# Two transformer layers on one core: loads in order of use, three dense units instead of four, scatters of two units in turn, the last row's slot rows made in one go

## The chip, the cores and the metric

The kernel runs on one core of a Trainium2 chip. The metric is the device time of one execution in microseconds (us). A core has five engines that work beside each other: TensorE (PE, matrix products; its weight loads are listed as PEld), VectorE (DVE), ScalarE (ACT), GpSimd (POOL) and SyncE (SP), which here does nothing but issue DMA transfers. SP, ACT and POOL each have a queue of their own for the transfers that they issue. POOL alone issues the indirect ones: scatters and gathers by a list of row numbers.

## The reference

The input is x, four rows (batch entries) of 1024 tokens with 128 numbers each, in float32. Two layers are applied; each adds an attention and a mixture of experts to x, both computed from the same normalised x:

```python
x = L0_attn_x
xn = _layernorm(x, axis=-1)
x = x + _L0_attn_ref(xn, ...) + _L0_ffn_ref(xn, ...)
xn = _layernorm(x, axis=-1)
x = x + _L1_attn_ref(xn, ...) + _L1_ffn_ref(xn, ...)
return x
```

The first layer's attention has 16 query heads of 8 numbers and one key/value head. Its "ffn" is itself an attention, with 8 heads (H) of width 128 (P), whose values and outputs each come from 8 experts (E):

```python
gate_v = _get_sel_gate(x, sel_v_w, rs)   # sigmoid, the best 2 of 8, normalised, times route_scale
gate_o = _get_sel_gate(x, sel_o_w, rs)
q = jnp.einsum('bsd,hpd->bhsp', x, q_w.reshape(H, P, D))
k = jnp.einsum('bsd,hpd->bhsp', x, k_w.reshape(H, P, D))
xv = jnp.einsum('bsd,hedp->bshep', x, v_w.reshape(H, E, D, P))
v = jnp.einsum('bshep,bshe->bhsp', xv, gate_v)
att = jax.nn.softmax(jnp.einsum('bhqp,bhkp->bhqk', q, k) * SCALE, axis=-1)
ctx = jnp.einsum('bhqk,bhkp->bqhp', att, v)
weighted = ctx[:, :, :, None, :] * gate_o[..., None]
out = jnp.einsum('bshep,hepd->bsd', weighted, o_w.reshape(H, E, P, D))
```

Since a gate is zero for six of the eight experts, only two of the eight values of a token and head are needed.

The second layer has a linear attention (16 heads, 64 random features, FAVOR+) and an ordinary mixture of experts: a router picks 2 of 8 experts per token, each expert is 128 to 512, exact gelu, 512 to 128, and a shared expert of the same size is added for every token.

## The kernel before

**Units.** The first layer's expert attention is cut into 32 units, u = 8 b + h, one for each row b and head h. The loop over u (L1055) has an inner loop over n = 0 to 7 (L1057), one step for each 128 query tokens. A step writes the scores' two 128x512 products (ss, L940), their maximum (DVE, L945) and exponential (ACT, L947), transposes an earlier step's probabilities (pTp, L960, copied by DVE, L964, and ACT, L966), makes half of the context at n = 4 and at n = 0 of the next unit (cp, L972), and writes outputs: two products against eight experts (po, L993), each weighed by the output gates on DVE (g_o, L997), then summed over the experts by add_experts (DVE 128x512, L824; POOL 128x256, L825) and two more POOL additions (L1002, L1003). The first attention's work (attend(): mx L613 with its maximum nmh L619, sT L667, pT L674, ov L657) is woven between these.

**Values, dense.** The first DENSE = 4 units, all of row 0, compute the values of all eight experts for every token: switch_values (L827) makes two 128x512 products for each n (pv, L835), DVE multiplies each by the gates (gv, L839), add_experts adds the first half to the second on DVE (L824) and the quarters on POOL (L825), and a last POOL addition (L844) writes vs. All of g_o, gv and two other temporaries take turns in three buffers (tag "gs"). Unit 0's values are made in one burst at u = 0, n = 3; those of unit u + 1 during unit u by the table VALUES (at u = 0: four n at step 4, then LATER).

**Values, sorted.** The other 28 units compute only the two chosen experts. 16 scatters (8 n x 2 choices, L864, POOL) put each token's normalised row into sorted_v[u % 4] at a place that the tables give, so that tokens of one expert stand together. Groups of four 128-token blocks are then loaded by SP (group_load, L870, which also fetches each block's expert weights), transposed (xvT, L892) and multiplied (pg, L897 on), written to DRAM by SP, gathered back by 16 POOL transfers (L916) and combined with their gates by POOL (L931, L932). A unit's scatters are spread over the two units before it by the table PAIR (L1016), which serves two units at a time (v and v + 1, where v is u + 3 at odd and u + 2 at even u): within one step all scatters of the first unit come before all of the second. group_load of a unit starts two units ahead, at step 4. The places in sorted_v that no token takes must be zero: four transfers of 1.47 MB at the start clear the four buffers (L1046 to L1050).

**Startup.** The loads of L97 to L151 stand on SP's queue in the order of the text: x of row 0, the two halves of sel, rs, wq, four pieces of bq, wk, then 9 pieces of bk0 and 9 of keep, wv, bv, wo, bo; after them the q and k weights of unit 0 (load_scores(0), L1036) and its value weights (load_dense(0), L1037), the other rows of x (L1044), and the clears. The layernorm of row 0, its transposes (lnT, L240) and copies by ACT into xnT (L241), the product qkT (L801) and the queries qks (L816) are the first compute.

**Last row.** Between the layers each token's normalised row is scattered with its number and its share to sorted_x at the place of its expert, once for each of two choices (slot_rows, L328): for each, POOL normalises 128 tokens into a buffer xslot, of which there are two (L334), copies the token number (L339) and the share (L340), and scatters (L341). For rows 0 to 2 this happens during the units of the following rows. For row 3 it is the end of last_row (L1292): the row's layernorm, router, the tables of all experts, then slot_rows. last_row runs as an "aside", advanced twice for every step of the second layer's attention (L1749 to L1764); a "filler" beside it gives the shared expert for three rows, then drains what is left of the aside, then the experts, whose first act is to load the sorted tokens (xg, L1655; transposed at L1670). wide() (L1288) is a pool of seven buffers that the second layer uses.

**Order.** PE, SP and POOL run in the order of the text in the first layer; DVE and ACT are ordered by a scheduler. In the second layer only PE and SP keep the order of the text (L1174).

## Time and profile before

| | before |
|---|---|
| three plain runs, us | 3378.05, 3382.25, 3383.11 (median 3382.25) |
| the profiled execution, us | 3353.22 |
| its span, us | 3351.2 |
| mean granted TensorE clock | 0.975 of full speed |
| instructions | 48567 |
| DMA moved | 293.65 MB, 88 GB/s on average |

The profiled execution is one of its own, 29 us below the median of the plain ones; stages and durations below come from it. The units of the first layer run until about 2860 us of the span, the second layer from there to the end.

A line of the part with the groups of instructions reads so:

```profile
L864 POOL DMA_INDIRECT sorted_v<-xv,gates x448 | 446.8, 997 | 387.4 <-DMA sorted_v<-xv,gates 322.4
L825 POOL TENSOR_TENSOR g_o<-g_o 128x256 f32<-128x256 f32 x256 | 191.7, 749 | 459.6 <-DVE g_o L824 430.3
L997 DVE TENSOR_TENSOR g_o<-po,go 128x512 f32<-128x512 f32 x512 | 334.0, 683 | 44.3 <-POOL x L1003 21.9
```

The first is: line 864 of the kernel, on POOL, an indirect DMA that writes sorted_v from xv by numbers in gates, 448 times; busy 446.8 us in all, 997 ns each; before them POOL stood idle for 387.4 us, of which 322.4 ended when an earlier scatter into sorted_v landed. The busy time of a DMA instruction is what the issuing engine spends on it, not the transfer. A row of the windows has a stretch of the span, its length, the busy time (and the number of instructions) of PE, PEld, DVE, ACT and POOL in it, the granted clock, the share of the DMA engines' time, and GB/s. A row of the waits has engine, line, what it waited for, the total in us, how often, and the longest. A row of the timeline has start, duration, engine, line, instruction, and in brackets the engine's idle time before it and what ended it.

### The profile page before, as it was taken

The page shows a single profiled execution, that of the slowest core. Times are in us where ns is not written, and L with a number is a line of the kernel's source. Part 1 is how long each engine was busy: PE and PEld are TensorE (multiplying, and loading weights), DVE is VectorE, ACT ScalarE, POOL GpSimd, SP SyncE. Part 2 cuts the span into 40 slices and gives each one's busy share as a digit, 9 for nine tenths or more (in the row PEclk, how much of TensorE's full clock was granted, in tenths as well). Part 3 has the DMA queues.
Part 4 walks back from the last instruction along what each step waited for, and adds up shares of the span by engine and source line. Part 5 has one row for each costly group of instructions (what it writes and reads, how often), then busy time and mean ns, then how long its engine had stood idle before and what let it go on. Part 6 is the DMA issues. An engine that isn't in the chain of part 4 may idle for free. (4 is left out here: it accounts for less than half of the span.)

```text
span 3351.2 us, 48567 instructions
## 1 busy us (share of the span) xinstructions
PE 3161.5 (94%) x15286; PEld 1712.1 (51%) x15286; DVE 2450.3 (73%) x4726; ACT 1817.6 (54%) x3164; POOL 1865.9 (56%) x2351
## 2 busy tenths in 40 slices
PE   5899999999999999999899999999999999879998
PEld 3344544555545444555454455555455554447776
DVE  7998777776788767676878786767666645648886
ACT  2234555555555555555555555556556566346665
POOL 1344355666657666666467667765767644153333
PEclk9999999999999999999999999999999999889999
DMA  4122443433322223333132232332333220024445
GB/s 141 48 65 76 131 140 98 123 104 96 87 74 84 86 76 96 93 94 92 57 94 88 86 90 89 99 92 82 97 88 92 85 77 13 12 64 88 86 91 133
DMA packets 449333, 293.65 MB, mean 88 GB/s; under 512 B 41450, under 2 KB 422260, under 8 KB 449076
## 3 DMA queue, kind: packets, MB, share of 16 engines
q1 hardware_dynamic: 404884, 221.32, 23.5%
q0 software_dynamic: 41952, 68.16, 7.4%
q8 instruction: 122, 2.00, 0.2%
q10 hardware_dynamic: 2240, 1.07, 0.1%
q14 instruction: 135, 1.11, 0.1%
HBM read 176.29 MB, written 113.71 MB: 87 GB/s over the span
## 5 line engine op out<-in xcount | busy, mean ns | idle before, releaser
L619 DVE TENSOR_REDUCE nmh<-mx 128x1 f32<-128x512 f32 x1024 | 664.2, 682 | 272.8 <-PE mx L613 271.2
L864 POOL DMA_INDIRECT sorted_v<-xv,gates x448 | 446.8, 997 | 387.4 <-DMA sorted_v<-xv,gates 322.4
L674 ACT ACTIVATE pT<-sT 128x512 f32<-128x512 f32 x1024 | 557.2, 600 | 164.4 <-PE sT L667 94.2
L940 PE MATMUL ss<-xnT,qTs 128*128 128x512 f32 x1024 | 493.4, 604 | 7.1 <-DVE g_o L997 2.6
L945 DVE TENSOR_REDUCE nms<-ps 128x1 f32<-128x1024 f32 x256 | 311.0, 1215 | 255.1 <-ACT ps L943 254.0
L972 PE MATMUL cp<-pTs,vs 128*128 128x512 f32 x1024 | 458.9, 602 | 21.2 <-DVE pTs L964 18.1
L993 PE MATMUL po<-ow,cTs 128*128 128x512 f32 x1024 | 474.4, 596 | 0.7 <-ACT cTs L977 0.7
L825 POOL TENSOR_TENSOR g_o<-g_o 128x256 f32<-128x256 f32 x256 | 191.7, 749 | 459.6 <-DVE g_o L824 430.3
L943 ACT COPY ps<-ss 128x512 f32<-128x512 f32 x512 | 299.4, 586 | 254.0 <-PE ss L940 250.9
L947 ACT ACTIVATE ps<-ps,nms 128x1024 f32<-128x1024 f32 x256 | 294.4, 1150 | 159.2 <-DVE nms L945 158.1
L997 DVE TENSOR_TENSOR g_o<-po,go 128x512 f32<-128x512 f32 x512 | 334.0, 683 | 44.3 <-POOL x L1003 21.9
L667 PE MATMUL sT<-qs,ks 75*128 75x512 bf16 x1024 | 310.6, 384 | 13.2 <-DVE nmh L619 9.3
L613 PE MATMUL mx<-ks,qs 72*128 72x512 bf16 x1024 | 312.9, 383 | 10.7 <-DVE nmh L619 4.9
L972 PEld LDWEIGHTS cp<-pTs,vs 128*128 128x128 f32 x1024 | 192.8, 193 | 245.7 <-issue 229.5
L960 PE MATMUL pTp<-ident,ps 128*128 128x128 f32 x2048 | 273.9, 277 | 12.5 <-ACT ps L947 8.8
L940 PEld LDWEIGHTS ss<-xnT,qTs 128*128 128x128 f32 x1024 | 190.1, 192 | 186.4 <-issue 105.1
L960 PEld LDWEIGHTS pTp<-ident,ps 128*128 128x128 f32 x2048 | 243.2, 143 | 81.4 <-issue 17.4
L993 PEld LDWEIGHTS po<-ow,cTs 128*128 128x128 f32 x1024 | 179.7, 191 | 158.8 <-issue 127.4
L977 ACT COPY cTs<-cp 128x512 f32<-128x512 f32 x64 | 37.4, 585 | 409.2 <-PE cp L972 403.0
L916 POOL DMA_INDIRECT vs<-yv,gates x224 | 219.2, 979 | 67.1 <-issue 56.1
L916 POOL DMA_INDIRECT yg<-yv,gates x224 | 216.6, 967 | 68.3 <-issue 68.0
L657 PE MATMUL ov<-pT,va 128*32 128x512 f32 x2048 | 248.4, 603 | 0.0
(314 smaller groups left out, 4826.8 us busy)
## 6 DMA issues: line engine op xcount, KB each, us to landing
vb<-in_v_w_dram SPq DMA_DIRECT2D x644, 64.0 KB
xs<-sorted_v SPq DMA_DIRECT2D x140, 256.0 KB
yv<-xs SPq DMA_DIRECT2D x140, 256.0 KB
w<-in_w_dram SPq DMA_DIRECT2D x78, 256.0 KB
sorted_x<-nobody SPq DMA_DIRECT2D x16, 1040.0 KB
ow<-in_o_w_dram SPq DMA_DIRECT2D x32, 512.0 KB
qs<-qd SPq DMA_DIRECT2D x144, 64.0 KB
sorted_v<-xv,gates POOLq DMA_INDIRECT x448, 2.3
```

Of the source, the lines that this page charges most:

```text
L613: nc.tensor.matmul(sc, lhsT=qs[0:NPAIR, i, ts(n, P)], rhs=ks[0:NPAIR, ts(kc, 512)], start=True, stop=True,)
L619: nc.vector.tensor_reduce(halves[:, i, n, kc : kc + 1], sc, axis=AX.X, op=ALU.max)
L667: nc.tensor.matmul(sc, lhsT=ks[:, ts(kt, P)], rhs=qs[:, i, ts(c, 512)], start=True, stop=True,)
L674: nc.scalar.activation(pT, sc, AF.Exp)
L864: nc.gpsimd.indirect_dma_start(out=sorted_v[u % 4][:, :], out_offset=bass.IndirectOffsetOnAxis(ap=column(u, k, n).bitcast(I32), axis=0), i ...
L916: nc.gpsimd.indirect_dma_start(out=to[:, n, :], out_offset=None, in_=unit[u, "y"][:, :], in_offset=bass.IndirectOffsetOnAxis(ap=column(u, ...
L940: nc.tensor.matmul(sc, lhsT=qT[:, ts(n, P)], rhs=xnT[b][:, ts(c, 512)], start=True, stop=True)
L945: nc.vector.tensor_reduce(nm, p, axis=AX.X, op=ALU.max, negate=True)
L960: nc.tensor.transpose(pt[:, ts(k, P)], p[:, ts(4 * k4 + k, P)], ident)
L972: nc.tensor.matmul(cp, lhsT=v[:, kt, :], rhs=pT[:, kt, :], start=(kt == 0), stop=(kt == NT - 1),)
L993: nc.tensor.matmul(po, lhsT=cT[:, ts(qt, P)], rhs=unit[u, "ow"][:, ts(c, 512)], start=True, stop=True,)
L997: nc.vector.tensor_tensor(g[:, ts(c, 4), :], po.rearrange("p (e c) -> p e c", e=4), bcast(go[:, ts(c, 4)], P), ALU.mult,)
```

## The change

- **Loads.** After x of row 0, the order on SP is now: q and k weights of unit 0, the two halves of sel (load_gates), wq, wk, the odd pieces of bk0 and keep, wv, bv, wo, bo (load_small), the value weights of unit 0. rs, the four pieces of bq and the pieces of bk0 and keep with even j (6 of bk0 and 6 of keep) are issued by ACT.
- **Dense units.** DENSE is 3: unit 3 is sorted. In the three dense units DVE weighs the first product of each n as before; the second is weighed by ACT, four instructions of 128x128 with a scale per token. The first addition of add_experts is done by POOL for the values of units 0 and 1, by DVE for unit 2 and for all outputs. The values of unit 2 are made at steps 1 to 4 of u = 1, two n per step.
- **Scatters.** Unit 3's 16 scatters are issued in the first four steps of u = 1, four each; PAIR_1 places those of units 4 and 5 in u = 1 and 2. From then on PAIR holds as before, but within a step the scatters of the two units alternate.
- **Last row.** last_slots makes row 3's slot rows: eight DVE instructions and one ACT copy into two wide buffers, four POOL copies for all token numbers and shares, and then 16 scatters, one for each advance of the aside. The aside is advanced three times per step for the first 15 advances and two times after.

```diff
@@ -42,3 +42,3 @@
 VG = 4
-DENSE = 4
+DENSE = 3
 
@@ -111,22 +111,7 @@
     sel = fixed([P, 2 * SH * SE], "sel")
-    nc.sync.dma_start(sel[:, 0 : SH * SE], a["sel_vT"])
-    nc.sync.dma_start(sel[:, SH * SE :], a["sel_oT"])
     rs = fixed([P, 1], "rs")
-    nc.sync.dma_start(rs, a["route_scale"].unsqueeze(0).to_broadcast([P, 1]))
+    wq0, bq0 = fixed([P, D], "wq0"), fixed([P, 1], "bq0")
 
-    wq0 = fixed([P, D], "wq0")
-    nc.sync.dma_start(wq0, a["Wq0T"])
-    bq0 = fixed([P, 1], "bq0")
-    for g in range(NG):
-        nc.sync.dma_start(
-            bq0[ts(g, 4 * HD), :], a["bq0"][:, :, g].rearrange("i d -> (i d)").unsqueeze(1)
-        )
-
-    wk0 = fixed([P, NSTACK], "wk0")
+    wk0, bk0 = fixed([P, NSTACK], "wk0"), fixed([NSTACK, 1], "bk0")
     nc.gpsimd.memset(wk0[:, NPAIR:], 0.0)
-    nc.sync.dma_start(
-        wk0[:, 0:NPAIR].rearrange("e (r d) -> e r d", d=HD),
-        a["Wkv0T"][:, 0:HD].unsqueeze(1).to_broadcast([P, NPAIR // HD, HD]),
-    )
-    bk0 = fixed([NSTACK, 1], "bk0")
     nc.gpsimd.memset(bk0, 1.0)
@@ -137,16 +122,32 @@
     nc.gpsimd.memset(minus1, -1.0)
-    for i in range(NPART):
-        for j in range(NPART):
-            r = 24 * i + HD * j
-            nc.sync.dma_start(bk0[r : r + HD, :], a["bkv0"][0:HD].unsqueeze(1))
-            for k in range(j):
-                nc.sync.dma_start(keep[r : r + HD, k : k + 1], minus1[0:HD, 0:1])
-    wv0 = fixed([P, HD], "wv0")
-    nc.sync.dma_start(wv0, a["Wkv0T"][:, HD : 2 * HD])
-    bv0 = fixed([P, HD], "bv0")
-    nc.sync.dma_start(bv0, a["bkv0"][HD : 2 * HD].unsqueeze(0).to_broadcast([P, HD]))
-    wo0 = fixed([P, D], "wo0")
-    nc.sync.dma_start(wo0, a["Wo0T"])
-    bo0 = fixed([P, D], "bo0")
-    nc.sync.dma_start(bo0, a["bo0"].unsqueeze(0).to_broadcast([P, D]))
+    wv0, bv0 = fixed([P, HD], "wv0"), fixed([P, HD], "bv0")
+    wo0, bo0 = fixed([P, D], "wo0"), fixed([P, D], "bo0")
+
+    def load_gates():
+        nc.sync.dma_start(sel[:, 0 : SH * SE], a["sel_vT"])
+        nc.sync.dma_start(sel[:, SH * SE :], a["sel_oT"])
+        nc.scalar.dma_start(rs, a["route_scale"].unsqueeze(0).to_broadcast([P, 1]))
+
+    def load_small():
+        nc.sync.dma_start(wq0, a["Wq0T"])
+        nc.sync.dma_start(
+            wk0[:, 0:NPAIR].rearrange("e (r d) -> e r d", d=HD),
+            a["Wkv0T"][:, 0:HD].unsqueeze(1).to_broadcast([P, NPAIR // HD, HD]),
+        )
+        for g in range(NG):
+            nc.scalar.dma_start(
+                bq0[ts(g, 4 * HD), :],
+                a["bq0"][:, :, g].rearrange("i d -> (i d)").unsqueeze(1),
+            )
+        for i in range(NPART):
+            for j in range(NPART):
+                r = 24 * i + HD * j
+                queue = (nc.scalar, nc.sync)[j % 2]
+                queue.dma_start(bk0[r : r + HD, :], a["bkv0"][0:HD].unsqueeze(1))
+                for k in range(j):
+                    queue.dma_start(keep[r : r + HD, k : k + 1], minus1[0:HD, 0:1])
+        nc.sync.dma_start(wv0, a["Wkv0T"][:, HD : 2 * HD])
+        nc.sync.dma_start(bv0, a["bkv0"][HD : 2 * HD].unsqueeze(0).to_broadcast([P, HD]))
+        nc.sync.dma_start(wo0, a["Wo0T"])
+        nc.sync.dma_start(bo0, a["bo0"].unsqueeze(0).to_broadcast([P, D]))
 
@@ -323,3 +324,3 @@
         yield from weigh(comb[:, b, :, 0:ME], oh0, share[:, 0, b, :], oh1, share[:, 1, b, :])
-        to_slots[b] = slot_rows(b, at_slot)
+        to_slots[b] = slot_rows(b, at_slot) if b < B - 1 else (moments[1, b], at_slot)
 
@@ -821,5 +822,5 @@
 
-        def add_experts(g):
+        def add_experts(g, engine):
 
-            nc.vector.tensor_tensor(g[:, 0:4, :], g[:, 0:4, :], g[:, 4:8, :], ALU.add)
+            engine.tensor_tensor(g[:, 0:4, :], g[:, 0:4, :], g[:, 4:8, :], ALU.add)
             nc.gpsimd.tensor_tensor(g[:, 0:2, :], g[:, 0:2, :], g[:, 2:4, :], ALU.add)
@@ -838,7 +839,16 @@
                 )
-                nc.vector.tensor_tensor(
-                    g[:, ts(c, 4), :], pv.rearrange("p (e c) -> p e c", e=4),
-                    bcast(gates[b][:, n, ds(h * SE + 4 * c, 4)], P), ALU.mult,
-                )
-            add_experts(g)
+                if c == 0:
+                    nc.vector.tensor_tensor(
+                        g[:, 0:4, :], pv.rearrange("p (e c) -> p e c", e=4),
+                        bcast(gates[b][:, n, ds(h * SE, 4)], P), ALU.mult,
+                    )
+                else:
+                    for e in range(4, SE):
+                        i = h * SE + e
+                        nc.scalar.activation(
+                            g[:, e, :], pv[:, ts(e - 4, P)], AF.Copy,
+                            scale=gates[b][:, n, i : i + 1],
+                        )
+
+            add_experts(g, nc.gpsimd if u < 2 else nc.vector)
             nc.gpsimd.tensor_tensor(v[:, n, :], g[:, 0, :], g[:, 1, :], ALU.add)
@@ -1000,3 +1010,3 @@
                 )
-            add_experts(g)
+            add_experts(g, nc.vector)
             nc.gpsimd.tensor_tensor(g[:, 0, :], g[:, 0, :], g[:, 1, :], ALU.add)
@@ -1012,3 +1022,3 @@
         LATER = {5: (4,), 6: (5,), 7: (6, 7)}
-        VALUES = {2: (0,), 3: (1, 2), 4: (3,), **LATER}
+        VALUES = {1: (0, 1), 2: (2, 3), 3: (4, 5), 4: (6, 7)}
 
@@ -1019,2 +1029,7 @@
         )
+
+        PAIR_1 = (
+            (0, 0, 0, 0, 3, 3, 3, 3, 1, 1, 1, 1, 0, 0, 0, 0),
+            (0, 0, 0, 0, 0, 0, 0, 0, 2, 2, 2, 2, 2, 2, 2, 2),
+        )
         GATHER = {13: (0,), 14: (1,), 15: (2,), 16: (3, 4), 17: (5,), 18: (6, 7)}
@@ -1036,2 +1051,4 @@
         load_scores(0)
+        load_gates()
+        load_small()
         load_dense(0)
@@ -1130,7 +1147,19 @@
                 v = u + 3 if odd else u + 2
+                if u == 1 and n < 4:
+                    for i in range(4 * n, 4 * n + 4):
+                        scatter(DENSE, i)
                 if u > 0 and v < U:
-                    for k, counts in enumerate(PAIR):
+
+                    pair = []
+                    for k, counts in enumerate(PAIR_1 if u < 3 else PAIR):
                         done = sum(counts[: n + 8 * (1 - odd)])
-                        for i in range(done, done + counts[n + 8 * (1 - odd)]):
-                            scatter(v + k, i)
+                        pair.append([
+                            (v + k, i)
+                            for i in range(done, done + counts[n + 8 * (1 - odd)])
+                        ])
+                    pair.sort(key=len, reverse=True)
+                    for i in range(len(pair[0])):
+                        for of_unit in pair:
+                            if i < len(of_unit):
+                                scatter(*of_unit[i])
 
@@ -1154,3 +1183,3 @@
                     for k in list(to_slots):
-                        if k < B - 1 and next(to_slots[k], to_slots) is to_slots:
+                        if next(to_slots[k], to_slots) is to_slots:
                             del to_slots[k]
@@ -1291,2 +1320,31 @@
 
+    def last_slots(moments_b, at_slot):
+
+        mv, rstd = moments_b
+        b = B - 1
+        to = [
+            wide(f"xlast{k}")[:, 0 : NT * ROW].rearrange("p (n d) -> p n d", d=ROW)
+            for k in range(2)
+        ]
+        for n in range(NT):
+            nc.vector.tensor_scalar(
+                to[0][:, n, 0:D], x[b][:, n, :], mv[:, n, 0:1], rstd[:, n : n + 1],
+                ALU.subtract, ALU.mult,
+            )
+        nc.scalar.copy(to[1][:, :, 0:D], to[0][:, :, 0:D])
+        for k in range(2):
+            nc.gpsimd.tensor_copy(
+                to[k][:, :, D].bitcast(I32), token[:, b * NT : (b + 1) * NT]
+            )
+            nc.gpsimd.tensor_copy(to[k][:, :, D + 1], share[:, k, b, :])
+        yield
+        for n in range(NT):
+            for k in range(2):
+                nc.gpsimd.indirect_dma_start(
+                    out=sorted_x[:, :],
+                    out_offset=bass.IndirectOffsetOnAxis(ap=at_slot[:, k, n : n + 1], axis=0),
+                    in_=to[k][:, n, :], in_offset=None,
+                )
+                yield
+
     def last_row():
@@ -1297,3 +1355,3 @@
         yield
-        yield from to_slots[B - 1]
+        yield from last_slots(*to_slots[B - 1])
 
@@ -1749,3 +1807,3 @@
     filler = fill()
-    due = 0.0
+    due, taken = 0.0, 0
     for k, (rows_now, rate) in enumerate((
@@ -1756,4 +1814,5 @@
         for _ in run(*its):
-            next(aside, None)
-            next(aside, None)
+            for _ in range(3 if taken < 15 else 2):
+                next(aside, None)
+                taken += 1
             due += rate
```

## Prediction

> **What bounds the kernel now.** I read the totals and the slices first, then the busy time by stage, then what TensorE (PE) waited for, and last the timeline of the three places that the change touches.
>
> ```profile
> PE 3161.5 (94%) x15286; PEld 1712.1 (51%) x15286; DVE 2450.3 (73%) x4726; ACT 1817.6 (54%) x3164; POOL 1865.9 (56%) x2351
> PE   5899999999999999999899999999999999879998
> DVE  7998777776788767676878786767666645648886
> ```
>
> PE is busy 94% of the span, so only 190 us of idle PE can be won, plus whatever PE work is removed. The slices show where it idles: the first two (168 us) and the last rows before the experts (slices 35 and 36).
>
> ```profile
> 0.00:84.00 84.00, 49.46 (x148) 25.75 (x149) 62.51 (x139) 18.48 (x30) 14.35 (x45) 0.92 0.49 141
> 84.00:168.00 84.00, 70.47 (x204) 31.17 (x203) 75.83 (x164) 20.81 (x36) 27.79 (x42) 0.94 0.17 48
> 168.00:252.00 84.00, 76.59 (x254) 37.78 (x253) 78.41 (x141) 26.04 (x44) 39.85 (x56) 0.96 0.20 65
> 252.00:336.00 84.00, 79.91 (x314) 38.31 (x312) 70.63 (x117) 39.17 (x71) 41.39 (x57) 0.96 0.27 79
> 2000.00:2500.00 500.00, 495.43 (x2315) 256.74 (x2315) 349.32 (x657) 296.16 (x543) 336.31 (x423) 1.00 0.31 91
> 2900.00:3000.00 100.00, 77.03 (x411) 41.89 (x410) 47.51 (x132) 41.96 (x50) 38.50 (x70) 0.81 0.12 35
> ```
>
> Columns: stretch, its length, busy PE, weight loads, DVE, ACT, POOL, then granted clock, DMA share, GB/s. Until 252 us DVE is as full as PE or fuller (75.8 and 78.4 of 84 in the second and third rows), ACT is a quarter busy: there DVE sets the pace, and PE idles 34.5+13.5+7.4 = 55 us. At 2000 us PE has 495 of 500: nothing but less PE work helps there.
>
> ```profile
> PE cp L972 <- DVE pTs L964: 18.1, 10, 5.3
> PE xgT L1670 <- DMA xg<-sorted_x: 13.7, 2, 12.0
> PE qkT L801 <- DMA qk<-in_q_wT_dram: 8.8, 1, 8.8
> POOL sorted_v L864 <- DMA sorted_v<-xv,gates: 322.4, 183, 5.3
> ```
>
> Total, times, longest. The first is DVE's lateness in the dense units, the second the last row's scatters, the third the startup load, the fourth scatters that wait for the one before into the same tensor.
>
> **Loads in order of use.**
>
> ```profile
> 7.07 0.80 SPq L143 DMA_DIRECT2D keep<-minus  x1
> 18.50 0.43 SPq L774 DMA_DIRECT2D qk<-in_q_wT_dram  x1
> 21.25 0.72 PE L801 MATMUL qkT<-ident,qk 128*128 128x128 f32 x2 [8.84 <-DMA qk<-in_q_wT_dram]
> 23.76 3.75 PE L816 MATMUL qks<-xnT,qkm 128*128 128x512 f32 x4 [0.47 <-DVE qkm L809]
> ```
>
> The weights of unit 0 are issued at 18.5 behind the small loads, and land 2.75 us later. Issued just behind x, they land before the layernorm's transposes end (12.4), so the whole 8.84 could go. But 12 of the little bk0/keep loads go to ACT ahead of its two copies of xnT (11.43 and 12.45 to 13.04), and each waits for an earlier DMA of its lane, four at a time. A DMA's way from issue to landing is 2.3 (the scatters' row) to 2.75 (qk): after rstd (ends 9.47) two such rounds and four issues of 0.45 make 6.4 to 7.3, so the first copy starts at about 16.3 and qks at about 17.2: -6.5. Smallest gain -4 (one more round), greatest -8.8 (the whole wait). SP sends the same number of bytes as before; the four clears of sorted_v (1.47 MB each, 16.09 us of issue from 23.92) move about 9 us earlier and lie behind the same unit 0 work, whose x and weights are ahead of them.
>
> **Dense units: half to ACT, adds of units 0 and 1 to POOL.** From DVE go 24 multiplies of 0.68 (L839) = 16.3, and 16 adds of 0.76 (L824) = 12.2. ACT gains 96 instructions of 128x128; the only row of that shape, mk L1427, takes 0.31: 29.8 us where ACT is 25% busy, hidden; were it not, about 1.2 per n against 0.68 saved. POOL gains 16 adds 128x512 of 1.06 (L931) to 1.37 (L932 where gaps are dense): 17 to 22 us. Unit 0's eight n come in one burst: on DVE 8 x 2.12 = 17 us before; on POOL now 8 x (1.37+0.75+0.48) = 21. POOL is then the slow one in that burst, so its gain is small: I take -3 for all of u = 0 on top of the startup, 0 to -8 (half of DVE's 23 us for units 0 and 1, less the POOL surplus).
>
> The Trainium skill's page "SBUF — State Buffer", section "Who interferes with whom", speaks against this step: a DVE instruction with two SBUF inputs contends with a GpSimd one that reads SBUF, and the loser waits it out. The trace's row for such a DVE add, L824, is 643/683/3127 ns (least, median, most) while POOL is over half busy, so a block exists but is rare. By the rule 16 POOL adds of 1.37 could cost DVE 22 us and the step would be worth nothing; by the row the cost is near 1 us. I go by the row.
>
> **Unit 3 sorted instead of dense.** PE loses 16 matmuls of 0.86 = 13.8 us and gets six groups of 1.33 (transposes and products of sorted blocks) = 7.9: -5.9, in a part that is 95% PE-busy (fourth row): it counts nearly in full, -6. From DVE go 16 x 0.68 + 8 x 0.76 = 17 us, partly beyond PE's bound: 0 to -8 more; I take -1. POOL gets 16 scatters (one DMA each), 16 gathers of 0.97 and 2 combines (2 x 1.06 + 1.37), SP the group loads and the yv writes of unit 3. In u = 2 and 3 POOL has room (41 of 84).
>
> **The scatters in u = 1** are the price.
>
> ```profile
> 149.50 1.21 POOL L864 DMA_INDIRECT sorted_v<-xv,gates  x1 [0.17 <-issue]
> 152.22 0.96 POOL L864 DMA_INDIRECT sorted_v<-xv,gates  x1 [1.51 <-DMA sorted_v<-xv,gates]
> 153.49 1.08 POOL L864 DMA_INDIRECT sorted_v<-xv,gates  x1 [0.30 <-issue]
> ```
>
> A scatter into the tensor of the one before starts 0.97 + 1.51 = 2.48 later; into another tensor 0.97 + 0.30 = 1.27. In u = 1 there are now 16 for unit 3 and 12 for unit 4, each in a row of its own tensor: 28 x 2.48 = 69. POOL also has eight output tails (0.72+0.46+0.45 = 1.7 each, 13.6) and the eight tails of unit 2's values (0.75+0.48, 9.9): 93 us. u = 1 lasted 149.5 to 246 = 96.5, with DVE full; DVE now has 8 x 0.68 = 5.4 less, so 91. POOL becomes the bound at about 93 to 98 (steps 1 to 3 need 9.9 + 1.7 + 2.5 = 14.1 against 12 on average; later steps 9.1 don't give that back when DVE needs 11): the change in u = 1 is 0, between -4 and +6. Queued behind the scatters on POOL are the g_o and gv sums, which free the three buffers that DVE's multiplies write, which free PE's po and pv banks. On SP the first group load of unit 3 (step 4) waits for the sixteenth scatter, and the qs and nmT loads of the first attention (L597, L643) lie behind it.
>
> **Scatters in turn, from u = 3.** They save up to 183 waits of about 1.2 on POOL, but PE is 99% busy there and waits for POOL nowhere for more than 1 us: 0, at best -4 (row changes).
>
> **The last row.**
>
> ```profile
> 2946.26 1.09 POOL L341 DMA_INDIRECT sorted_x<-xslot,at_slot  x1 [0.98 <-DMA sorted_x<-xslot,at_slot]
> 2949.57 1.09 POOL L341 DMA_INDIRECT sorted_x<-xslot,at_slot  x1 [1.11 <-DMA sorted_x<-xslot,at_slot]
> 2987.78 0.66 PE L1670 MATMUL xgT<-ident,xg 128*128 128x128 f32 x2 [12.01 <-DMA xg<-sorted_x]
> ```
>
> Sixteen scatters go from 2932.6 to 2982.9, 3.3 apart, and each already waits about 1 us for the one before to land: the slot row (0.79+0.18+0.17) is hidden in that wait. They all still go into sorted_x, so making the rows ahead takes nothing off while the landing stays at 3.2; at the 2.48 of L864 it takes 15 x 0.8 = 12. On the other side the first scatter now waits for eight DVE instructions, an ACT copy (0.58 to 1.15) and four POOL copies (0.18 each): 8 x 0.27 + 1 + 0.7 = 4, and for the DVE work queued ahead of them, about 3: +4 to +7. Taking the aside three per step brings the chain forward by 0 to 5. Net 0, between -12 and +6.
>
> **Sum.** -6.5 - 3 - 7 + 0 + 0 + 0 = -16.5, on the profiled 3353.2 (span 3351.2): 3336.7. The three plain runs have the median 3382.25, 29 above it, so the forecast is 3382.25 - 16.5, about 3366. A change within 0.2%, 6.8 us, can't be told from none.
>
> **Rivals.**
> 1. POOL takes over in u = 1 outright and the change is slower. The scatters of that stage (84 to 260 us) land after 2.2 to 3.4 us, median 2.8. If the spacing is 3.4, POOL needs 28 x 3.4 + 23.5 = 119, +22; with SP's loads held behind the group load for one more step (+8) that is +30, less the 16.5 of the sum: +13, 3395. It decides from a spacing of about 2.9. Against it: the measured spacing in this stage is 2.7 and 2.48. Chance 0.22.
> 2. The gains before u = 1 are all handed back, since POOL is the last in u = 1 whatever comes before it, and only unit 3's PE work counts, against a last row that starts 6 late: -6.5 + 6 + 0, 3382. For: 93 against 91 is near. Against: POOL can only start its scatters when u = 1 starts, so an earlier start stays. Chance 0.14.
> 3. Everything pays: startup -8.8, u = 0 -8, unit 3 -8, the last row -6: -31, 3351. For it: PE idles 55 us in the first 252. Chance 0.12.
> 4. The ready slot rows do not do what they say: the chain keeps its 3.3 and starts 6 late. Alone that gives 3382.25 - 16.5 + 6 = 3372, inside the forecast case, so it has no chance of its own.
>
> **How the numbers follow.** The forecast case, 3357 to 3375, has 0.52. Faster is it and case 3, 0.64; same 0.14; slower 0.22. The range goes from 3352 (case 3) to 3390 (most of the way to case 1).
>
> **What would show it.** In the changed profile: PE's first qks at about 17 instead of 23.8, and xnT copies behind ACT's DMA issues; the first scatter of u = 1 near 140 instead of 149.5; u = 1 with POOL over 90% busy and a wait of DVE or PE for POOL's sums; one pass less of PE work for unit 3 before 340; the last row's scatters still over 3 apart and xgT near 2972, the same 16 early. I am wrong if u = 1 takes over 105 us, if the last row's scatters fall to 2.5 apart, or if PE's idle time between 60 and 260 does not fall.

## The result

The changed kernel takes 3371.39 us (median of 13 runs, 3365.72 to 3379.76), the kernel before beside it 3386.09 (13 runs). The ratio is 0.9964 with a 95% interval of 0.9951 to 0.9976: -12.2 us, between -16.6 and -8.1. The forecast was -16.5.

The profiled execution of the changed kernel has a span of 3368.5 us, longer than the 3351.2 of the profile shown before. That earlier profile was quicker than any of the 13 runs beside it: a second profile of the same kernel has a span of 3383.9 (run before_again). The two agree within 0.2 us on the start of unit 5 (521.0 and 520.8 us), and within 0.5 us on the second layer (562.6 and 562.1 from the start of unit 31); the 33 us lie between, where the change touches nothing but the order of the scatters. So stages are compared below up to unit 5 and from unit 31 on, and the stretch between them, where one kernel differs by more than the change is worth, with caution.

The page of the changed kernel, totals and two of the slice rows:

```profile
PE 3174.4 (94%) x15323; PEld 1718.9 (51%) x15323; DVE 2417.9 (72%) x4670; ACT 1852.0 (55%) x3273; POOL 1897.1 (56%) x2345
...
PE   6889999999999999999899999999999999889998
...
DVE  6787786767778767666868876667666655658886
```

Against the first profile of the kernel before, PE is busy for 13 us more, against the second (3176.4) for 2 less, at nearly the same clock (0.973 and 0.972): of the 6 us of PE work that the forecast took away little is to be seen. DVE has 32 us less than in the first profile, ACT 34 more, POOL 31 more. The windows of the same kernel (columns as before: stretch, length, PE, PEld, DVE, ACT, POOL, clock, DMA share, GB/s):

```profile
0.00:84.00 84.00, 52.27 (x160) 27.88 (x160) 58.59 (x135) 29.37 (x64) 22.75 (x53) 0.89 0.56 152
84.00:168.00 84.00, 73.73 (x196) 32.80 (x195) 66.33 (x137) 30.68 (x71) 41.81 (x53) 0.88 0.14 38
168.00:252.00 84.00, 74.24 (x260) 40.05 (x259) 71.52 (x127) 33.95 (x73) 46.44 (x62) 0.92 0.26 82
252.00:336.00 84.00, 78.10 (x344) 40.51 (x343) 60.37 (x101) 45.39 (x83) 42.46 (x52) 0.94 0.45 131
```

DVE is relieved as planned (66.3 instead of 75.8 in the second row, 71.5 instead of 78.4 in the third), POOL takes it over (41.8 instead of 27.8), and PE is busy for 6 us more in the first two rows together and 4 less in the last two: a new wait has come in, and the granted clock is lower (0.88 instead of 0.94, 0.92 instead of 0.96). The waits of the changed kernel:

```profile
PE lnT L241 <- DVE xn L234: 17.3, 4, 10.8
...
PE cp L982 <- DVE pTs L974: 10.3, 9, 2.7
...
PE pTp L970 <- DVE gv L841: 8.5, 2, 6.8
...
PE xgT L1728 <- DMA xg<-sorted_x: 2.4, 2, 2.2
```

The wait for qk (8.8) is gone, the one for the sorted tokens is down from 13.7, and a single wait of 6.8 for a multiply of values by gates (gv) has come.

### The profile page after: what moved, and what is told of

Same layout as the page of the kernel before. It is cut to its first block, busy times and chain, and to the rows that moved or that the text cites. A ratio compares the mean times of both kernels' runs of the same rounds, so it can differ in the third digit from the quotient of the medians.

```text
span 3368.5 us, 48933 instructions
## 1 busy us (share of the span) xinstructions
PE 3174.4 (94%) x15323; PEld 1718.9 (51%) x15323; DVE 2417.9 (72%) x4670; ACT 1852.0 (55%) x3273; POOL 1897.1 (56%) x2345
## 5 line engine op out<-in xcount | busy, mean ns | idle before, releaser
L874 POOL DMA_INDIRECT sorted_v<-xv,gates x464 | 466.1, 1005 | 334.0 <-DMA sorted_v<-xv,gates 247.1
L970 PEld LDWEIGHTS pTp<-ident,ps 128*128 128x128 f32 x2048 | 242.6, 143 | 90.4 <-issue 18.3
L926 POOL DMA_INDIRECT vs<-yv,gates x232 | 228.5, 985 | 67.5 <-issue 59.4
L926 POOL DMA_INDIRECT yg<-yv,gates x232 | 224.2, 967 | 73.7 <-issue 73.4
```

Of the source, the lines that this page charges most:

```text
L874: nc.gpsimd.indirect_dma_start(out=sorted_v[u % 4][:, :], out_offset=bass.IndirectOffsetOnAxis(ap=column(u, k, n).bitcast(I32), axis=0), i ...
L926: nc.gpsimd.indirect_dma_start(out=to[:, n, :], out_offset=None, in_=unit[u, "y"][:, :], in_offset=bass.IndirectOffsetOnAxis(ap=column(u, ...
L970: nc.tensor.transpose(pt[:, ts(k, P)], p[:, ts(4 * k4 + k, P)], ident)
```

## The experiments

Twelve runs followed, in three groups on three chips (A, B, C); each is compared with the kernel before on its own chip (3386.2 us, 3387.2 and 3364.5). On which chip the changed kernel and the first profile ran is not on record. "Start of a unit" is the start of DVE's first row maximum (nms) in it, read from the traces:

| kernel | chip | ratio to before (95%) | us | unit 1 starts | unit 2 | unit 5 |
|---|---|---|---|---|---|---|
| before (first profile / before_again) | - / B | 1 | 0 | 148.5 / 148.3 | 234.0 / 234.7 | 521.0 / 520.8 |
| changed | - | 0.9964 (0.9951 to 0.9976) | -12.2 | 147.6 | 240.5 | 519.0 |
| loads_only | A | 0.9979 (0.9963 to 0.9994) | -7.1 | 144.3 | 230.1 | 519.0 |
| adds_dve | A | 0.9932 (0.9918 to 0.9946) | -23.0 | 140.6 | 234.4 | 514.2 |
| dense4 | A | 0.9946 (0.9932 to 0.9961) | -18.3 | 148.3 | 229.6 | 511.8 |
| last_as_before | A | 0.9968 (0.9954 to 0.9983) | -10.8 | 147.6 | 240.5 | 518.7 |
| dense4_adds | B | 0.9955 (0.9939 to 0.9971) | -15.2 | 142.5 | 224.3 | 507.4 |
| dense4_adds_noact | B | 0.9948 (0.9929 to 0.9967) | -17.6 | 144.1 | 230.3 | 511.9 |
| u1_turns | B | 0.9970 (0.9957 to 0.9984) | -10.2 | 148.0 | 242.3 | 521.4 |
| turns_only | C | 0.9956 (0.9940 to 0.9973) | -14.8 | 150.3 | 236.9 | 520.4 |
| no_turns | C | 0.9971 (0.9959 to 0.9983) | -9.8 | 146.6 | 240.6 | 516.7 |
| dense4_adds_loads2 | C | 0.9909 (0.9894 to 0.9925) | -30.6 | 142.1 | 223.7 | 506.1 |
| dense4_adds_2 | C | 0.9901 (0.9886 to 0.9917) | -33.3 | 142.2 | 224.1 | 505.2 |

The column us is the ratio less 1, times the time before on that chip. The start of unit 5 is repeatable within some 2 us (changed, last_as_before: the same first layer, 519.0 and 518.7; dense4_adds and dense4_adds_2, the same kernel on two chips: 507.4 and 505.2), so it tells parts of more than that apart, which the times, at some 5 us of interval to each side, can't.

### before_again

The kernel before, unchanged.

> The kernel before once more, unchanged, for a second profile. The one at hand ran 3353 us where the plain runs have a median of 3386, while the profiles of all variants lie within 4 us of their plain medians. If that profile was one lucky execution, this one has a span of 3370 to 3390, and its units 24 to 31 take as long as the variants' (83.4 us each, not 82.6); if the profile is always shorter for this kernel, about 3352.

The span is 3383.9 us, and units 24 to 30 take 83.5 us each (2237.5 to 2821.8), so the first profile was the odd one beside the times of chips A and B. Another chip could be the reason too: on chip C the kernel before takes 3357.8 to 3370.0. Both profiles have nearly the same windows up to 336 us (PE busy for 276.4 and 277.2 us of 336), where most readings of the prediction lie, and nearly the same last row (waits of PE for xg of at most 12.0 and 12.5).

### loads_only

The kernel before with the load part of the change:

```diff
         load_scores(0)
+        load_gates()
+        load_small()
         load_dense(0)
...
+                queue = (nc.scalar, nc.sync)[j % 2]
+                queue.dma_start(bk0[r : r + HD, :], a["bkv0"][0:HD].unsqueeze(1))
```

> The kernel before with the new order of loads and nothing else. My theory: the first queries start 6.5 us earlier (17.2 instead of 23.8) and since DVE is full behind them nearly all of it stays: -5 to -7 us against before. Rival: the saving is used up by the clears, which now collide with unit 0's loads, or by DVE, which had slack to catch up: within 2 us of before.

-7.1 us (-12.5 to -2.0), and unit 1 starts 4 us earlier. By the time this is the first theory. By the mark that repeats it is nearer the rival: unit 2 starts 3.9 to 4.6 us earlier, unit 5 only 1.8 to 2.0. Whether more than 2 us of the earlier start stay is not settled. How the start looks in the changed kernel's timeline (start, duration, engine, line, instruction, in brackets the idle time before it and its end):

```profile
15.18 1.38 ACTq L148 DMA_DIRECT2D keep<-minus  x2
...
16.61 1.07 ACT L242 COPY xnT<-lnT 128x512 f32<-128x512 f32 x2 [6.59 <-DMA keep<-minus]
17.25 3.78 PE L817 MATMUL qks<-xnT,qkm 128*128 128x512 f32 x4 [2.54 <-ACT xnT L242]
```

The copies stand behind ACT's own DMA issues for 6.59 us, and the queries begin at 17.25 instead of 23.76.

### adds_dve

```diff
-            add_experts(g, nc.gpsimd if u < 2 else nc.vector)
+            add_experts(g, nc.vector)
```

> The changed kernel with the first addition of units 0 and 1 back on DVE; ACT keeps its half. In the trace of the changed kernel the burst of unit 0's values runs at 2.56 us per n on POOL (1.27 + 0.73 + 0.46 and gaps), DVE waits for it six times. Theory: POOL took over in the burst, so moving the addition back makes the burst 8 x 1.45 = 11.6 instead of 20.5 us, and gives up to 8 us less in unit 0, of which 12 x 0.76 us of DVE work come back where DVE is full: -3 us against the changed kernel, -15 against before. Rival: the relief of DVE is what the gain comes from: +6 against the changed kernel, -6 against before.

-23.0 us, 10.8 better than the changed kernel, and unit 1 starts 7.0 earlier. The burst of unit 0's values in the changed kernel, one n after the other on POOL, with DVE's multiply of a later n:

```profile
69.86 1.27 POOL L825 TENSOR_TENSOR gv<-gv 128x512 f32<-128x512 f32 x1
...
71.20 0.72 POOL L826 TENSOR_TENSOR gv<-gv 128x256 f32<-128x256 f32 x1
72.00 0.45 POOL L854 TENSOR_TENSOR vs<-gv 128x128 f32<-128x128 f32 x1
72.42 1.27 POOL L825 TENSOR_TENSOR gv<-gv 128x512 f32<-128x512 f32 x1
72.49 0.69 DVE L841 TENSOR_TENSOR gv<-pv,gates 128x512 f32<-128x512 f32 x1 [1.21 <-POOL vs L854]
```

One n takes 72.42 - 69.86 = 2.56 us, POOL has no gap, and DVE, which was to be relieved, waits for POOL's last sum to give back a buffer. The same burst with the addition on DVE:

```profile
74.47 0.73 POOL L826 TENSOR_TENSOR gv<-gv 128x256 f32<-128x256 f32 x1
75.28 0.87 POOL L854 TENSOR_TENSOR vs<-gv 128x128 f32<-128x128 f32 x1
76.11 0.72 POOL L826 TENSOR_TENSOR gv<-gv 128x256 f32<-128x256 f32 x1
```

1.64 us for one n. Eight n at 0.92 less are 7.4, the 7.0 by which unit 1 starts earlier.

### dense4

```diff
-DENSE = 3
+DENSE = 4
...
-                if u == 1 and n < 4:
-                    for i in range(4 * n, 4 * n + 4):
-                        scatter(DENSE, i)
...
-                    for k, counts in enumerate(PAIR_1 if u < 3 else PAIR):
+                    for k, counts in enumerate(PAIR):
```

> The changed kernel with four dense units: unit 3 dense again (made during u = 2, its half weighed by ACT), the old table of scatters from u = 1 on, with the scatters of two units still in turn. Theory: unit 3 sorted takes 5.9 us of PE work away, so without it +6 against the changed kernel, -6 against before. Rival: the 28 scatters of u = 1 on POOL cost as much as the PE work saves: same as the changed kernel, -12 against before, or -18 if they cost more.

-18.3 us: the rival with the larger cost. Unit 1 lasts 81.3 us (148.3 to 229.6) instead of the changed kernel's 92.8, while units 2 and 3 together last 4.2 longer (187.0 instead of 182.8, to the start of unit 4 at 416.6 and 423.3). So with unit 3 sorted units 2 and 3 are 4 us shorter, and u = 1 is 11.5 longer. Where the 11.5 are, in the changed kernel's timeline:

```profile
185.85 0.99 POOL L874 DMA_INDIRECT sorted_v<-xv,gates  x1 [0.16 <-issue]
188.68 0.96 POOL L874 DMA_INDIRECT sorted_v<-xv,gates  x1 [1.85 <-DMA sorted_v<-xv,gates]
191.19 0.96 POOL L874 DMA_INDIRECT sorted_v<-xv,gates  x1 [1.55 <-DMA sorted_v<-xv,gates]
193.68 0.96 POOL L874 DMA_INDIRECT sorted_v<-xv,gates  x1 [1.53 <-DMA sorted_v<-xv,gates]
...
196.01 0.45 POOL L1013 TENSOR_TENSOR x<-x,g_o 128x128 f32<-128x128 f32 x1
...
196.50 0.69 DVE L841 TENSOR_TENSOR gv<-pv,gates 128x512 f32<-128x512 f32 x1 [8.12 <-POOL x L1013]
...
197.24 1.97 PE L970 MATMUL pTp<-ident,ps 128*128 128x128 f32 x8 [6.81 <-DVE gv L841]
```

Four scatters keep POOL from 185.85 to 194.66. An output's sums stand behind them (their g_o add on DVE had ended at 187.8), and only at 196.5 do they give back the buffer for which the multiply of unit 2's values waits; DVE stands 8.12 us, and PE 6.81 us for the bank (the buffer for its products) that this multiply empties. And it does not end there. The windows from 184 to 196 and 196 to 208 us of the changed kernel:

```profile
184.00:196.00 12.00, 6.43 (x20) 2.73 (x18) 4.37 (x9) 1.73 (x5) 6.67 (x9) 0.86 0.20 66
196.00:208.00 12.00, 10.76 (x34) 7.71 (x35) 8.42 (x13) 5.23 (x14) 7.72 (x11) 0.58 0.04 17
```

and the same two windows of dense4:

```profile
184.00:196.00 12.00, 12.00 (x53) 7.08 (x52) 12.00 (x21) 5.88 (x15) 6.31 (x10) 1.00 0.84 250
196.00:208.00 12.00, 12.00 (x37) 5.77 (x36) 11.53 (x19) 4.54 (x12) 6.68 (x8) 1.00 0.42 138
```

In the second window of the changed kernel the granted clock is 0.58, where dense4 has 1.00 in both. Cut finer, it is 0.50 from 192.5 to 206.2 us, so it falls 2 us after PE has begun to wait and stays there for 9.0 us after PE works again. At half the clock these 9.0 us do the work of 4.5, so the wait costs 6.8 + 4.5 = 11.3 us (an estimate from these rows), nearly all of the 11.5. The other four runs with three dense units have the same 13.7 us at 0.50 in u = 1 (between 187.8 and 207.9), and none of the nine with four dense units leaves the full clock between 160 and 220 us.

### last_as_before

```diff
-        yield from last_slots(*to_slots[B - 1])
+        yield from to_slots[B - 1]
...
-            for _ in range(3 if taken < 15 else 2):
+            for _ in range(2):
```

(slot_rows for all rows again.)

> The changed kernel with the last row's slot rows made and scattered as before, two advances of the aside per step. Theory: the scatters' chain is set by the landing of each, so the ready rows bring nothing: 0 against the changed kernel, -12 against before. Rival: the wait of PE for xg (12.0 us before, 2.2 after in the profiles) was worth its length: +8 to +10 against the changed kernel, -3 against before.

-10.8 us, 1.4 from the changed kernel and within the intervals: the number of the first theory. The stretch from the start of unit 31 to the end agrees: on chips A and B and in the first profiles it takes 560.6 to 565.9 us with the new slot rows and 562.1 to 565.8 without, on chip C 556.9 to 558.1 and 557.7. The theory's reason does not hold, though, since the chain did get shorter. In the changed kernel's timeline two of the sixteen scatters, and the product that waited for them:

```profile
2959.54 0.97 POOL L1343 DMA_INDIRECT sorted_x<-xlast,at_slot  x1 [2.11 <-DVE cTs L1665]
2962.09 0.97 POOL L1343 DMA_INDIRECT sorted_x<-xlast,at_slot  x1 [1.58 <-DMA sorted_x<-xlast,at_slot]
2965.16 0.97 POOL L1343 DMA_INDIRECT sorted_x<-xlast,at_slot  x1 [2.10 <-DMA sorted_x<-xlast,at_slot]
...
3000.70 0.41 PE L1728 MATMUL xgT<-ident,xg 128*128 128x128 f32 x2 [0.18 <-DMA xg<-sorted_x]
```

The distances are now 2.55 and 3.07 in turn. The sixteen go from 2952.5 to 2996.0, 43.5 us instead of 50.3, 2.9 apart instead of 3.35. Counted from the start of unit 31, the first comes at 145.1 (before: 144.0 and 140.0 in the two profiles; last_as_before 143.5), xgT at 193.3 (199.2, 195.5; 198.5) and the end at 561.1 (562.6, 562.1; 565.8). The longest wait of PE for xg fell from 12.0 to 2.2 us, but xgT comes only 2 to 6 us earlier, since PE gets there later: part of its waiting has moved ahead, to the last row's layernorm (lnT for xn 5.8 us between 2800 and 3010 us, where the kernel before has no wait of this kind). The length of the wait is no measure of what it cost.

### dense4_adds and dense4_adds_2

Both of the better choices together: the diffs of adds_dve and dense4. First group B:

> The changed kernel with both undone: four dense units, and the first addition on DVE. Alone each was faster than the changed kernel (-11 us the addition on DVE, -6 us four dense units). Theory: one cost POOL time in the bursts of u = 0, the other in u = 1, so they add: -29 us against before. Rival: both relieve the same wait for POOL, and with four dense units DVE has 8 more additions: no better than the addition alone, -23 against before.

It measured -15.2 us (-20.7 to -9.8), against both theories, though unit 5 starts at 507.4, 11.6 before the changed kernel's, near the sum of 4.8 (adds_dve) and 7.2 (dense4). So it ran again, on chip C:

> Four dense units and the first addition on DVE, the same kernel as in the run dense4_adds, once more. Its start of unit 5 was 13.5 us ahead of the kernel before, as the two parts alone add up to (6.6 and 9.0), but its time only 15 us, not 29. If the parts add up and that was chance of the later units: -19 to -29 now. If the time is really no better than that of either alone: -11 to -19 again.

-33.3 us (-38.4 to -27.9), 3329.2 against 3364.5. The two intervals of one kernel do not touch. Up to unit 5 the two executions are alike (507.4, 505.2); from unit 8 to unit 31 they take 2048.6 and 2007.9 us with the same instructions, and no single wait of PE there accounts for it (PE is busy for 1974.7 and 1959.6 us, so some 26 us more of idle PE and 15 of longer work). What makes that stretch differ is not settled. That the parts add up to unit 5 is shown; that the version is faster than the kernel before is shown on chips B and C. Whether it is faster than the changed kernel is open: on chip B its ratio is not told apart from the changed kernel's, and on chip C the changed kernel was not timed.

### dense4_adds_noact

```diff
-                if c == 0:
-                    nc.vector.tensor_tensor(
-                        g[:, 0:4, :], pv.rearrange("p (e c) -> p e c", e=4),
...
-                else:
-                    for e in range(4, SE):
-                        i = h * SE + e
-                        nc.scalar.activation(
...
+                nc.vector.tensor_tensor(
+                    g[:, ts(c, 4), :], pv.rearrange("p (e c) -> p e c", e=4),
```

> The same, and DVE weighs both halves of every product as in the kernel before (ACT none): 32 multiplies of 0.68 us back on DVE. Theory: DVE sets the pace until 330 us, so ACT's half is worth 8 to 16 us: -13 to -21 against before. Rival: the earlier loads and the dense values spread over the steps bring the gain, and ACT's half nothing: -27 to -31 against before.

-17.6 us, no worse than dense4_adds beside it (-15.2); unit 5 starts 4.5 later. So ACT's half is worth 4.5 us up to unit 5, which is less than these times can tell, and not the 8 to 16 of the first theory; the time falls into that theory's numbers only since dense4_adds itself came out far from its own. Of DVE's 32 x 0.68 = 22 us most are not on the path.

### u1_turns

```diff
-            (0, 0, 0, 0, 3, 3, 3, 3, 1, 1, 1, 1, 0, 0, 0, 0),
+            (3, 3, 3, 3, 0, 0, 0, 0, 1, 1, 1, 1, 0, 0, 0, 0),
...
+                    if u == 1 and n < 4:
+                        pair.append([(DENSE, i) for i in range(4 * n, 4 * n + 4)])
```

> The changed kernel, with unit 4's first twelve scatters moved to the first four steps of u = 1 and issued in turn with unit 3's sixteen. A pair into two tensors takes 2.5 us like a single one, so 28 x 2.5 = 70 us of scatters on POOL become about 16 x 2.5 = 40. Theory: with unit 3 sorted, u = 1 lasts 92.8 us instead of 81.3 since POOL's scatters hold the sums back, so this takes some 4 to 8 us off the changed kernel: -16 to -20 against before. Rival: it is the number of waits in the first steps that costs, which stay at four a step: 0 against the changed kernel, -12 against before.

-10.2 us, and unit 1 lasts 94.3 instead of 92.8: the rival's number, but not its reason. POOL's waits for scatters in unit 1 fell from 28.6 to 6.2 us, and PE's wait for gv stayed (7.7). So it is not the sum of POOL's work and waits in u = 1 that costs. What has stayed is the row of scatters ahead of the sums in one step, now seven instead of four but still about 9 us long (188.15 to 197.25); a version with shorter rows was not tried.

### turns_only and no_turns

turns_only is the kernel before with this alone, no_turns the changed kernel without it:

```diff
+                    pair.sort(key=len, reverse=True)
+                    for i in range(len(pair[0])):
+                        for of_unit in pair:
+                            if i < len(of_unit):
+                                scatter(*of_unit[i])
```

> The kernel before, with the scatters of the two units of a step issued in turn and nothing else. My prediction gave this 0, at best -4 us: PE waits for POOL almost nowhere after u = 3. Rival: the profiles of the versions with the turns gain 6 to 13 us on the second profile of the kernel before between units 8 and 31 (mean 9), the one with the loads alone gains nothing there; if that is the turns' work, -6 to -10 against before. The start of unit 5 (521 us) moves by less than 1 in both cases.

> The changed kernel with the scatters of a step one unit after the other, as before. If the turns bring nothing: -12 against before, as the changed kernel. If they bring 6 to 10: -2 to -6 against before.

turns_only -14.8 us (-20.2 to -9.1), no_turns -9.8 (-13.8 to -5.7). Taking turns alone is worth 9 us or more on chip C, no less than all the rest of the change without it. The start of unit 5 hardly moves (520.4), so the gain lies later. POOL's waits for the scatter before sum up to 218.9 us in turns_only's profile and to 357.0 in that of no_turns. No profile of the kernel before was taken on chip C, and the changed kernel was not timed there, so where the gain lies, and how much of it is in the changed kernel, stays open: the ones that have the turns on chips A and B leave little room for 15 us (last_as_before -10.8, u1_turns -10.2). The stretch from unit 8 to unit 31, where the versions differ in the turns alone, points to a gain there. On chips A and B it takes 2043.3 and 2044.1 us without them (loads_only, before_again) and 2034.4 to 2039.7 with them in five of six runs, on chip C 2019.4 without (no_turns) and 2007.9 to 2015.8 with them. But dense4_adds has the turns and took 2048.6, and the first profile has none and took 2014.1, so with one profile of each it is not shown.

### dense4_adds_loads2

dense4_adds with

```diff
-                queue = (nc.scalar, nc.sync)[j % 2]
+                queue = nc.sync
```

> The changed kernel with four dense units, the first addition on DVE, and all pieces of bk0 and keep issued by SP, so that ACT copies xnT at once. ACT's copies start at about 12 instead of 16.6, the queries at about 15 (qkm is ready then) instead of 17.2, the start of unit 5 comes 2 us earlier than with four dense units and the addition on DVE alone (507.4): 505. Time: 2 us below that version, -17 to -30 against before. Rival: DVE, full from 30 us on, has other work late then and hides it: 507, same time.

Its timeline has the copies and the queries where they were expected:

```profile
11.98 0.59 ACT L242 COPY xnT<-lnT 128x512 f32<-128x512 f32 x1 [1.95 <-PE lnT L241]
...
15.19 2.04 PE L817 MATMUL qks<-xnT,qkm 128*128 128x512 f32 x2 [0.48 <-DVE qkm L810]
```

But the 2.0 us that it is ahead at the start of unit 0 (29.4 against the 31.4 of dense4_adds_2) are down to 0.1 at the start of unit 1, unit 5 starts at 506.1 against 505.2, and the time is 3332.7 against 3329.2: the rival. That it is DVE that hides the 2 us, being full from 32 to 60 us (27.96 of 28 in the changed kernel), is the likely reason and was not tried apart.

## Why the prediction was near in sum, and not in its parts

**Loads in order of use (-6.5): the start right, the worth open.** The first copy was put at 16.3 and the queries at 17.2; they are at 16.61 and 17.25. Alone this measured -7.1 by the time, and 1.8 to 2.0 by the start of unit 5. The prediction took all of the earlier start as gain; of the next 2 us (dense4_adds_loads2) nothing was left at unit 1.

**Dense units ("-3 for all of u = 0 on top of the startup, 0 to -8"): wrong.** Unit 0 begins 4.4 to 5.4 us earlier and unit 1 only 0.7 to 0.9: about 4 us are lost in u = 0. The prediction had the price of one n on POOL (1.37 + 0.75 + 0.48 = 2.6; measured 2.56) and said that POOL is then the slow one, but counted part of DVE's relief as a gain all the same. In this burst, which goes from one engine to the next over three buffers, the slowest set the pace, and the relief of the others brought nothing: 8 x (2.56 - 1.64) is the whole of what adds_dve wins in unit 0. The warning that was drawn from the Trainium skill's page "SBUF — State Buffer" was the smaller matter: with the addition on DVE, its sixteen instructions up to 150 us have a median of 692 ns and a longest of 1748, so long ones are seldom; on POOL the median is 1268. What decided was that difference. The skill's page "GPSIMD Engine Reference", section "3.1 Elementwise — side-by-side cycle accounting", has a float32 addition of N = 2048 1.96 times as long on GpSimd as on DVE. The traces, at 128x512, nearly agree with 1268 to 692, 1.8 times.

**Unit 3 sorted, and the scatters in u = 1 (-6 - 1 + 0): wrong.** Against four dense units the net is a loss, 7.2 us at the start of unit 5 (519.0 - 511.8) and 6.1 by the times (18.3 - 12.2, with intervals that overlap). The saving was put too high (4.2 measured), but the step that failed is u = 1, "0, between -4 and +6": it lasts 92.8 us, against 81.3 with unit 3 dense and 85.5 and 86.4 in the kernel before. The stretch that the prediction took for u = 1, 149.5 to 246 = 96.5, ends 12 us after unit 2 has begun (234.0), so the room that it gave POOL's 93 us was not there. Nor did POOL need them: between 148 and 240 us it is busy for 43.7, waits 28.6 for scatters to land and some 17 for DVE, and takes 24 of the 28 scatters. What is queued behind the scatters, the g_o sums, the buffers, the multiplies and PE's banks, was named in the right order. What was left out is that the order on POOL can cost what its sum does not: four scatters in a row, 8.8 us, ahead of one output's sums are enough to stop PE for 6.81 us, with the clock at half for 9.0 us after it. The first rival had the right place and the wrong cause, scatters further apart; within a row of four they are 2.5 to 2.8 apart.

**Scatters in turn ("0, at best -4"): wrong where it was tried alone**, -14.8 on chip C. The prediction looked for waits of PE for POOL and found none; the way from POOL's waits to the end it did not find, and neither did the runs.

**The last row (net 0): right in sum.** 1.4 us by the times, and nothing to be seen from unit 31 to the end. That the scatters would still be over 3 apart was wrong (2.9 on average), so the chain is 7 us shorter; that they would start later was right by 1 to 5 us. That a chain shorter by 7 us would bring the end no nearer was not in the prediction, which took such a gain at its full length.

**The sum.** By the start of unit 4 the forecast was ahead by all of its 16.5; measured, the changed kernel is ahead by 3.6 to 4.9 there (423.3 against 426.9 and 428.2), and by 1.8 to 2.0 at the start of unit 5. Most of the difference is unit 3 and the burst of unit 0: with both undone unit 5 starts 13.4 to 15.8 us ahead (dense4_adds and dense4_adds_2). The other 10 us or so of the measured 12.2 lie behind unit 5, where the prediction had nothing; turns_only makes the turns the likeliest source, which is argued and not shown. So the time was met by luck: two losses and a gain, none of which the prediction had, nearly cancel. One of its own signs of error did show: of the 200 us from 60 to 260 PE is busy for 171.2, and it was 170.2 and 171.6 before, so its idle time did not fall. Nor did the first scatter of u = 1 come near 140: it starts at 147.8.

## What to carry to other kernels

Work that is moved from a full engine to an idle one has to be checked at the point where both work on the same buffers: the slower of the two set the pace of the burst here, whatever the averages said. On an engine that runs in order, look for the longest row of instructions ahead of one that others wait for, and not only at the sum of a stage; to put such a row behind that instruction, or to cut it up, is the next thing to try, and was not tried here. Where the same kernel differs by more between executions than the change is worth, a mark that repeats well (here the start of unit 5, within some 2 us) tells parts apart that the times don't. A number that comes out as a theory has it does not show the theory's reason: the last row and u1_turns met the number for another reason.

## What the runs showed of the hardware that was not expected

- The same kernel ran 3386.2, 3387.2 and 3364.5 us on three chips, and a ratio to it is not the same on each: dense4_adds has 0.9955 (0.9939 to 0.9971) on one and 0.9901 (0.9886 to 0.9917) on another.
- The wait of PE of 6.81 us costs about 11: the granted clock is 0.50 for 13.7 us, of which PE works for 9.0. The Trainium skill's page "TensorE: Matmul & The Clock Gate", section "Part 1: The HAM clock gate (the "warmup" mystery)", says that the clock falls to half after at least one idle window of about 3.4 us and returns after at least one such window of work. The trace agrees that a wait of this length halves the clock; the return took 9.0 us of unbroken work, well over one such window.
- Without POOL work between them, scatters of the last row into sorted_x come 2.55 and 3.07 us apart in turn, those into sorted_v 2.5; with the slot rows made between them it was mostly 3.2 to 3.3, although POOL then stood idle for about 1 us before most of them. Why is open.
